# Layer 1's x with tokens on partitions: transposes of 32x32 squares on VectorE and transfers within SBUF in place of TensorE transposes

## The chip, the cores and the metric

The kernel runs on one core of one Trainium2 chip. TensorE multiplies matrices out of SBUF into PSUM; VectorE (DVE), ScalarE (ACT) and GpSimd (POOL) work elementwise on SBUF and PSUM; SyncE (SP) issues transfers, which 16 DMA engines carry out. SBUF has 128 partitions. The engines run side by side, each in the order of its own queue, and wait for one another by semaphores. The metric is the device time of one execution in microseconds, the median over several runs.

## The reference

Four layers are applied one after another to x of shape (4, 512, 32, 32) in float32: 4 images of 512 channels and 1024 tokens. Layers 0, 2 and 3 are attention layers (8 heads, one head, 4 heads) with a residual. Layer 1, which the change touches, is linear attention:

```
Q = einsum('bcn,mc->bmn', xf, wq) + bq          # m = 64 features
K = einsum('bcn,mc->bmn', xf, wk) + bk
V = einsum('bcn,oc->bon', xf, wv) + bv
gate = (max(xf, -1) + mean(xf, -1))[:, :, None]
V = gate * V
Qf = softplus(Q).transpose(0, 2, 1);  Kf = softplus(K)
KV = einsum('bmn,bcn->bmc', Kf, V)
norm = 1 / einsum('bnm,bm->bn', Qf, sum(Kf, -1) + EPS)
wval = einsum('bnm,bmc,bn->bcn', Qf, KV, norm).reshape(b, c, h, w)
return x + gamma * wval
```

## The kernel before, in words

`plain_path` does the whole computation; a second path, `general_path`, follows only when a check of magnitudes at the end fails, and the change leaves it alone. An image lies in SBUF as 128 partitions x 4 chunks x 1024 tokens: channels on partitions. Two images fit at a time; `away` writes one to DRAM and `back` fetches one, both on SP's queue.

Layer 0 runs image by image: `project_qkv` (lines 707 and 832 of the matmul helpers, products of 2x2 blocks by seven multiplications), then `attention`. Layer 1 of image b-1 has no stage of its own. `linear_attention` returns a list of small steps, and `project_qkv` of image b takes one step from that list at each `slot()`, between its own matmuls. The first three images are treated so while Layer 0 projects the next image; Layer 1 of the fourth image rides on the first stage of Layer 2. TensorE's order is written out by hand through this list (`manual_schedule` covers TensorE alone); the order on DVE, ACT, POOL and SP is set by a scheduler when the program is built.

Layer 1 doesn't form V. It uses KV = (Kf x^T) wv^T + (sum of Kf) bv, so it needs x with tokens on partitions, as the moving operand of a product that sums over tokens. The steps of `linear_attention(b, scratch)`, in order:

- `gates`: maximum on DVE (L1414) and sum on ACT (L1417) of each channel; the ACT pass writes four copies nobody reads into scratch buffer 3.
- `features(0)`, `features(1)`: 128 rows of q and k features for 512 tokens each (L641), then `softplus` over both (L1385 to L1391), which uses scratch buffers 0, 1 and 2 as e, u and l. L1389 is the last reader of e, L1390 the last of u, L1391 the last of l.
- `transpose_x(0)` to `transpose_x(3)`: each takes 256 tokens, eight 128x128 transposes on TensorE (L1425) into a PSUM tile of two banks, and one copy to SBUF, on ACT for even pieces (L1432), on DVE for odd ones (L1430). Piece i goes to scratch buffer (i + 3) % 4, so piece 0 takes the one of the gates' copies, and pieces 1, 2 and 3 take e, u and l. `transpose_keys` (L1438) stands between pieces 2 and 3.
- `keys_times_x` (L1454): the product of the transposed keys with pieces 0 and 1 in one step, 2 and 3 in the next; then `sum_keys` (L1465), `divide_queries` (L1478, L1488, L1489, and the transfer L1492 that copies the divided queries to the other 64 partitions), `transpose_kx` (L1497), `keys_times_values` (L641 with wv1, L1513) and two `update` steps (L1520, L1526), which add to x.

For the first three images scratch buffers are the four v tiles of the image being projected, which are written later in the same stage; for the fourth they come from the pool of four pt tiles. `many_tile` is a pool of one tile of 128 x 2048 elements, used by the attention for sums of exponentials. At the start wv1, the weights of V, is loaded by one transfer (L599), 128 partitions x 4 chunks x 512, channel 128 c + p on partition p of chunk c. The attention's quotients pass through DRAM by L1030 and L1033, and L1051 multiplies by them before the projection of the outputs (L1084).

Of the kernel before, what the change touches and what calls it, by code (L numbers as in the profile page):

```python
# [18 lines left out]
P = 128  # L19
# [3 lines left out]
NC = C // P  # L23
NT = S // P
# [2 lines left out]
QT = TB // P  # L27
M = 64
GROUP = 16
LIMIT = 1e18  # L30


# [18 lines left out]
def general_path(ctx: ExitStack, tc: tile.TileContext, d: dict, out: bass.AP):  # L51
# [41 lines left out]
    for b in range(1, B):  # L93
# [19 lines left out]

    gmat = const.tile([P, P // GROUP, GROUP], F32, name="gmat")
    nc.vector.memset(gmat, 1.0 / GROUP)
    nc.gpsimd.affine_select(
        out=gmat, in_=gmat, pattern=[[-GROUP, P // GROUP], [0, GROUP]],
        compare_op=ALU.is_ge, fill=0.0, base=0, channel_multiplier=1,
    )
    nc.gpsimd.affine_select(  # L120
        out=gmat, in_=gmat, pattern=[[GROUP, P // GROUP], [0, GROUP]],
        compare_op=ALU.is_ge, fill=0.0, base=GROUP - 1, channel_multiplier=-1,
    )
# [351 lines left out]
def plain_path(ctx: ExitStack, tc: tile.TileContext, d: dict, out: bass.AP, count):  # L475
# [11 lines left out]
    nc = tc.nc  # L487
# [11 lines left out]
    def acc_tile():  # L499
        return ps_acc.tile([P, TB], F32, tag="acc", name="acc")  # L500

    def two_tile(name):
        return ps_sc.tile([P, 2, TB], F32, tag="sc", name=name)

    def row_tile(name):
        return work.tile([P, TB], F32, tag="row", bufs=3, name=name)
# [7 lines left out]
    def many_tile(name):  # L514
        return work.tile([P, NC, TB], F32, tag="many", name=name)
# [9 lines left out]
    def chunks_tile(tag, name, bufs=1):  # L525
        return work.tile([P, NC, TB], F32, tag=tag, bufs=bufs, name=name)
# [69 lines left out]


    wv1 = chunks_tile("xn", "wv1", 2)
    nc.sync.dma_start(wv1, d["wv1"].rearrange("(c p) o -> p c o", p=P))  # L599
    block1 = chunks_tile("xn", "block1", 2)  # L600
    wqk1 = block1[:, 0, :].rearrange("p (c o) -> p c o", c=NC)
    nc.sync.dma_start(wqk1, d["wqk1"].rearrange("(c p) o -> p c o", p=P))
# [10 lines left out]
    ident = const.tile([P, P], F32, name="ident")  # L613
# [9 lines left out]

    gmat = const.tile([P, P // GROUP, GROUP], F32, name="gmat")
    nc.vector.memset(gmat, 1.0 / GROUP)
# [767 lines left out]
    def linear_attention(b, scratch):  # L1393

        x = xs[b]
        t = {}
        flat = lambda tile: tile.rearrange("p a s -> p (a s)")
# [21 lines left out]
            nc.vector.tensor_scalar(gate, gate, gamma, None, ALU.mult)  # L1419

        def transpose_x(i):
            ps = two_tile("xt")
            for s in range(2):
                for c in range(NC):
                    nc.tensor.transpose(  # L1425
                        ps[:, s, bass.ts(c, P)], x[:, c, bass.ts(2 * i + s, P)], ident
                    )
            t["xt", i] = scratch((i + 3) % 4)
            if i % 2:
                nc.vector.tensor_copy(t["xt", i], ps)  # L1430
            else:
                nc.scalar.copy(t["xt", i], ps)  # L1432

        def transpose_keys():

# [12 lines left out]
        def keys_times_x(i):  # L1448
            if i == 0:
                t["kx"] = acc_tile()  # L1450
            xt = t.pop(("xt", i))

            for s in range(2):
                nc.tensor.matmul(  # L1454
                    t["kx"][s * M : (s + 1) * M, :], lhsT=t["kf"][:, 2 * i + s, :],
                    rhs=xt[:, s, :], start=(i == 0), stop=(i == NT // 2 - 1),
                )
            if i == NT // 2 - 1:
                kx = row_tile("kx")
                nc.scalar.copy(kx, t["kx"])  # L1460
                t["kx"] = kx
# [53 lines left out]
        def update(tb):  # L1515
# [16 lines left out]
            lambda: features(0),  # L1532
            lambda: features(1),
            lambda: transpose_x(0),
            lambda: transpose_x(1),
            lambda: transpose_x(2),
            transpose_keys,
            lambda: transpose_x(3),
            both(lambda: keys_times_x(0), lambda: keys_times_x(1)),
            both(lambda: keys_times_x(2), lambda: keys_times_x(3), sum_keys),  # L1540
            divide_queries,
            transpose_kx,
# [103 lines left out]
    def verdict():  # L1646

        assert next(unit) <= UNITS
        ok = const.tile([P, 2 * UNITS], F32, name="ok")
        nc.vector.tensor_scalar(ok, tops.rearrange("p a n -> p (a n)"), LIMIT, None, ALU.is_le)  # L1650
        row = const.tile([P, 1], F32, name="row")
# [6 lines left out]
    with tc.manual_schedule(engines={mybir.EngineType.PE}):  # L1658
# [73 lines left out]
        for o in range(NC):  # L1732
            ps = gps.get(o)
            if ps is None:
                ps = acc_tile()
# [5 lines left out]
        for o in range(NC):  # L1741
            ps = acc_tile()
# [113 lines left out]
@with_exitstack  # L1856
def conv_seq(ctx: ExitStack, tc: tile.TileContext, d: dict, out: bass.AP):
    nc = tc.nc
    flag = ctx.enter_context(tc.tile_pool(name="flag", bufs=1))
    count = flag.tile([1, 1], mybir.dt.int32, name="count")  # L1860
    plain_path(tc, d, out, count)
    good = nc.values_load(count, min_val=0, max_val=P)
    with tc.If(good < P):
        general_path(tc, d, out)
# [56 lines left out]
```

## Time and profile before

| | |
|---|---|
| median of 3 runs | 2451.55 us (2450.8 to 2452.09) |
| the profiled execution's own time | 2450.76 us |
| its span, first to last instruction | 2449.0 us |
| granted TensorE clock | 1.000 |
| TensorE busy | 2433.3 us, 99% of the span |
| VectorE busy | 1506.1 us, 61% |
| ScalarE busy | 704.6 us, 29% |
| GpSimd busy | 251.1 us, 10% |
| DMA queue of SP's issues | 9.9% of 16 engines' span |
| TensorE's transposes of x (L1425) | 128, 272 to 273 ns each |

The durations come from one profiled execution, whose own time is 0.8 us below the median. Busy time says how full an engine is; matmuls overlap, so the mean length of one (594 ns for 512 columns) is longer than the distance from one to the next, and what a group of them holds TensorE for is read from the starts in the timeline. Issues of transfers are not counted as busy; they are seen as instructions of SPq. A number after an arrow in brackets is the idle time of the engine just before, and what ended it.

### The profile page before, as it was taken

What the parts mean: (1) busy time and instruction counts of PE and PEld (TensorE: products, weight loads), DVE (VectorE), ACT (ScalarE), POOL (GpSimd) and SP (SyncE); (2) the same over time, 40 slices, a digit from 0 to 9 for tenths busy, and PEclk for the clock granted to TensorE, in tenths of its full rate; (3) what the DMA queues carried; (4) which work ended last, traced back from release to release, by engine and by line L of the source; (5) the groups of instructions that cost most, each with busy time, mean ns of one, the idle gap of its engine ahead of it and who ended that gap; (6) DMA issues with size and microseconds to landing.
All of it is one profiled execution on the core that took longest, in us unless ns stands there. A gap on an engine that the chain in (4) does not pass through costs nothing.

```text
span 2449.0 us, 24662 instructions
## 1 busy us (share of the span) xinstructions
PE 2433.3 (99%) x10098; PEld 1225.7 (50%) x10098; DVE 1506.1 (61%) x1798; ACT 704.6 (29%) x864; POOL 251.1 (10%) x240
## 2 busy tenths in 40 slices
PE   9999999999999999999999999999999999999999
PEld 4544544453455344644645446445556456555653
DVE  3677577757775788656595774763554554445344
ACT  1454144415531653221211201112321430332132
POOL 4001100110010001101103021021010001002000
PEclk9999999999999999999999999999999999999999
DMA  5000020002000301011001010110010001001001
GB/s 185 7 12 18 5 78 10 18 5 79 19 9 13 130 23 48 5 69 39 31 1 69 5 74 13 52 69 18 35 69 1 18 35 52 1 35 35 1 22 45
DMA packets 28959, 88.64 MB, mean 36 GB/s; under 512 B 2508, under 2 KB 10188, under 8 KB 25895
## 3 DMA queue, kind: packets, MB, share of 16 engines
q1 hardware_dynamic: 28838, 87.00, 9.9%
q8 instruction: 81, 1.33, 0.2%
q14 instruction: 40, 0.32, 0.0%
HBM read 60.59 MB, written 25.35 MB: 35 GB/s over the span
## 4 chain that ended last, share of the span: by engine, by line
PE 99%; DVE 1%; ACT 0%; issue 0%; DMA 0%; SPq 0%; DVEq 0%
PE acc L707 20%; PE acc L832 12%; PE acc L967 9%; PE acc L982 9%; PE sc L936 9%; PE sc L931 9%; PE acc L839 8%; PE acc L1084 7%; PE acc L1316 6%; PE acc L1277 2%; PE feat L641 1%; PE acc L1018 1%; PE acc L641 1%; PE upd L1520 1%; PE acc L1454 1%; PE xt L1425 1%
## 5 line engine op out<-in xcount | busy, mean ns | idle before, releaser
L941 ACT ACTIVATE pt<-sc 128x1024 f32<-128x1024 f32 x384 | 379.2, 1022 | 541.2 <-PE sc L936 304.0
L950 DVE TENSOR_TENSOR sum<-sum,pt 128x1024 f32<-128x1024 f32 x256 | 314.6, 1229 | 159.0 <-ACT pt L941 146.5
L967 PE MATMUL acc<-pt,v 64*64 64x512 f32 x2048 | 247.6, 591 | 0.0
L931 PE MATMUL sc<-q,k 64*64 64x512 f32 x2048 | 245.0, 591 | 1.1 <-ACT pt L941 1.1
L982 PE MATMUL acc<-pt,v 128*128 128x512 f32 x512 | 240.8, 594 | 0.0
L936 PE MATMUL sc<-q,k 128*128 128x512 f32 x512 | 239.9, 594 | 0.0
L707 PE MATMUL acc<-t,ws 128*128 128x512 f32 x384 | 173.9, 594 | 0.0
L695 POOL TENSOR_TENSOR ws<-wqkv 128x256 f32<-128x256 f32 (+1 forms) x40 | 39.7, 992 | 1307.1 <-PE acc L1018 523.2
L947 DVE TENSOR_TENSOR sum<-pt 128x1024 f32<-128x1024 f32 x64 | 78.0, 1219 | 137.4 <-ACT pt L941 137.4
L982 PEld LDWEIGHTS acc<-pt,v 128*128 128x128 f32 x512 | 96.8, 190 | 125.1 <-issue 121.4
L936 PEld LDWEIGHTS sc<-q,k 128*128 128x128 f32 x512 | 97.1, 191 | 115.9 <-issue 92.7
L967 PEld LDWEIGHTS acc<-pt,v 64*64 64x64 f32 x2048 | 78.3, 133 | 142.5 <-issue 140.3
L931 PEld LDWEIGHTS sc<-q,k 64*64 64x64 f32 x2048 | 77.3, 133 | 140.9 <-issue 131.9
L707 PEld LDWEIGHTS acc<-t,ws 128*128 128x128 f32 x384 | 72.6, 190 | 86.5 <-issue 85.0
L746 ACT COPY v<-acc 128x512 f32<-128x512 f32 x24 | 14.0, 585 | 308.6 <-PE acc L832 308.6
L678 DVE RECIPROCAL rd<-acc 128x512 f32<-128x512 f32 (+1 forms) x24 | 80.5, 3353 | 29.1 <-PE acc L1018 29.1
L832 PE MATMUL acc<-ws,t 128*128 128x256 f32 x384 | 87.3, 380 | 0.0
L839 PE MATMUL acc<-qs,w 128*128 128x512 f32 x192 | 86.6, 593 | 0.0
L839 PE MATMUL acc<-q,ln 128*128 128x512 f32 x192 | 85.8, 593 | 0.0
L1084 PE MATMUL acc<-ot,wo 128*128 128x256 f32 x336 | 80.7, 383 | 2.7 <-ACT ou L1103 2.7
L737 DVE TENSOR_TENSOR v<-acc,v 128x512 f32<-128x512 f32 x72 | 49.5, 689 | 51.5 <-PE acc L832 51.2
L746 ACT COPY q<-acc 128x512 f32<-128x512 f32 x40 | 23.4, 585 | 197.1 <-PE acc L707 197.1
(326 smaller groups left out, 3476.0 us busy)
## 6 DMA issues: line engine op xcount, KB each, us to landing
home<-x SPq DMA_DIRECT2D x8, 2048.0 KB
x<-home SPq DMA_DIRECT2D x8, 2048.0 KB
out<-x SPq DMA_DIRECT2D x32, 256.0 KB
rds<-quotients SPq DMA_DIRECT2D x30, 256.0 KB
rds<-quotients SPq DMA_DIRECT2D x7, 1024.0 KB
x<-in_x SPq DMA_DIRECT2D x3, 2048.0 KB
wo<-in_wo SPq DMA_DIRECT2D x3, 1024.0 KB
w<-in_w SPq DMA_DIRECT2D x1, 3072.0 KB
```

The source lines that it names most:

```text
L678: nc.vector.reciprocal(rd, ps)
L707: nc.tensor.matmul(ps, lhsT=w[:, m, :], rhs=x[:, m, :], start=start, stop=stop, skip_group_check=True)
L832: nc.tensor.matmul(ps[:, bass.ts(r, C // 2)], lhsT=x[:, m, bass.ts(2 * o + r, P)], rhs=w[:, m, :], start=(start and r == 0), stop=stop, sk ...
L839: nc.tensor.matmul(ps, lhsT=x[:, m, bass.ts(o, P)], rhs=w[:, m, :], start=start, stop=stop, skip_group_check=True,)
L931: nc.tensor.matmul(ps[half(h), s, :], lhsT=key(g, i)[half(s), half(h)], rhs=q[qb][half(s), g, :], start=True, stop=True,)
L936: nc.tensor.matmul(ps[:, s, :], lhsT=key(g, 2 * i + s), rhs=q[qb][:, g, :], start=True, stop=True)
L941: exps.append(nc.scalar.activation(pt, ps, AF.Exp, scale=scale).ins)
L950: adds.append(nc.vector.tensor_tensor(acc, acc, pt, ALU.add).ins)
L967: nc.tensor.matmul(outs[qb, g][r][half(s), :], lhsT=v[i // 2][half(r), i % 2, g * P + s * hd : g * P + (s + 1) * hd], rhs=pt[half(r), s, : ...
L982: nc.tensor.matmul(outs[qb, g][0], lhsT=v[j // 2][:, j % 2, bass.ts(g, P)], rhs=pt[:, s, :], start=(j == 0), stop=(j == NT - 1),)
L1084: nc.tensor.matmul(ps[i][:, bass.ts(o, n)], lhsT=w[:, m, bass.ts(o, P)], rhs=t[:, m, :], start=(start and m + o == 0), stop=(stop and m == ...
L1316: nc.tensor.matmul(ps[i, o], lhsT=w[m][:, bass.ts(o, P)], rhs=t[m], start=(start and m == 0), stop=(stop and m == 3), skip_group_check=True,)
```

## The change

`transpose_x` no longer uses TensorE or PSUM. DVE transposes every 32x32 square of 256 tokens x 512 channels in one instruction (4 per image) into half of a `many` tile named squares: pieces 0 and 2 use one half, 1 and 3 the other. A square's transpose stays in the 32 partitions that its channels came from, so SP then issues 16 transfers per piece, each of 32 partitions x 256 elements (32 KB), which put them together in the scratch buffer with 128 tokens on the partitions: 64 transfers per image. The channels and tokens come out in another order than before. `keys_times_x` reads its moving operand in runs of 32 elements for that, and wv1 is loaded in the matching order of rows, by four transfers of 32 partitions in place of one. ACT's and DVE's copies out of PSUM are gone with the transposes.

```diff
--- before.py
+++ after.py
@@ -27,6 +27,7 @@
 QT = TB // P
 M = 64
 GROUP = 16
+SQUARE = 32
 LIMIT = 1e18
 
 
@@ -596,7 +597,10 @@
 
 
     wv1 = chunks_tile("xn", "wv1", 2)
-    nc.sync.dma_start(wv1, d["wv1"].rearrange("(c p) o -> p c o", p=P))
+
+    rows = d["wv1"].rearrange("(c a j) o -> c j a o", c=NC, a=NC)
+    for c in range(NC):
+        nc.sync.dma_start(wv1[c * SQUARE : (c + 1) * SQUARE], rows[c])
     block1 = chunks_tile("xn", "block1", 2)
     wqk1 = block1[:, 0, :].rearrange("p (c o) -> p c o", c=NC)
     nc.sync.dma_start(wqk1, d["wqk1"].rearrange("(c p) o -> p c o", p=P))
@@ -1419,17 +1423,27 @@
             nc.vector.tensor_scalar(gate, gate, gamma, None, ALU.mult)
 
         def transpose_x(i):
-            ps = two_tile("xt")
-            for s in range(2):
-                for c in range(NC):
-                    nc.tensor.transpose(
-                        ps[:, s, bass.ts(c, P)], x[:, c, bass.ts(2 * i + s, P)], ident
-                    )
-            t["xt", i] = scratch((i + 3) % 4)
-            if i % 2:
-                nc.vector.tensor_copy(t["xt", i], ps)
-            else:
-                nc.scalar.copy(t["xt", i], ps)
+
+
+
+
+
+            if i == 0:
+                t["squares"] = many_tile("squares")
+            sq = t["squares"][:, i % 2 * 2 : i % 2 * 2 + 2, :].rearrange(
+                "p b (r n j) -> p (b r) n j", j=SQUARE, n=2 * NC
+            )
+            nc.vector.transpose(
+                sq.rearrange("p r n j -> p n r j"),
+                x[:, :, i * 2 * P : (i + 1) * 2 * P].rearrange("p c (n j) -> p c n j", j=SQUARE),
+            )
+            xt = t["xt", i] = scratch((i + 3) % 4)
+            to = flat(xt).rearrange("p (a f) -> p a f", a=NC)
+            part = lambda i: slice(i * SQUARE, (i + 1) * SQUARE)
+            for r, a in itertools.product(range(NC), range(NC)):
+                nc.sync.dma_start(
+                    to[part(r), a, :], sq[part(a), r].rearrange("p n j -> p (n j)")
+                )
 
         def transpose_keys():
 
@@ -1448,12 +1462,12 @@
         def keys_times_x(i):
             if i == 0:
                 t["kx"] = acc_tile()
-            xt = t.pop(("xt", i))
+            xt = flat(t.pop(("xt", i))).rearrange("p (b s j) -> p s b j", s=2, j=SQUARE)
 
             for s in range(2):
                 nc.tensor.matmul(
                     t["kx"][s * M : (s + 1) * M, :], lhsT=t["kf"][:, 2 * i + s, :],
-                    rhs=xt[:, s, :], start=(i == 0), stop=(i == NT // 2 - 1),
+                    rhs=xt[:, s], start=(i == 0), stop=(i == NT // 2 - 1),
                 )
             if i == NT // 2 - 1:
                 kx = row_tile("kx")
```

Lines of the changed kernel lie 4 higher after the load of wv1 and 14 higher after `transpose_x`.

## The prediction

> **What bounds the kernel now.** I read the page's busy times and its chain first, then TensorE's waits, then the timeline of one Layer 1 stage, then the list of SP's DMA issues.
>
> ```profile
> PE 2433.3 (99%) x10098; PEld 1225.7 (50%) x10098; DVE 1506.1 (61%) x1798; ACT 704.6 (29%) x864; POOL 251.1 (10%) x240
> ...
> PE 99%; DVE 1%; ACT 0%; issue 0%; DMA 0%; SPq 0%; DVEq 0%
> ```
>
> TensorE is busy for 2433.3 of 2449.0 us and the chain that ended last is 99% TensorE. So whatever leaves its queue is a gain of its full length, and whatever makes its queue wait is a loss of its full length; nothing else counts. The waits of TensorE amount to about 10 us over the whole run, none of them in Layer 1.
>
> The timeline of the second image's projection (Layer 1 of the first image rides on it), columns start, length, engine, line, operation:
>
> ```profile
> 218.61 1.29 DVE L1051 TENSOR_TENSOR ot<-ot,rds 128x512 f32<-128x512 f32 x2 [1.01 <-DMA rds<-quotients]
> 220.23 1.89 PE L1084 MATMUL acc<-ot,wo 128*128 128x256 f32 x8
> 240.64 0.18 ACT L1417 ACTIVATION_READ_ACCUMULATOR v<-x 128x1 f32 x1
> 251.46 0.69 DVE L1387 TENSOR_SCALAR v<-v 128x1024 f32<-128x1024 f32 x1 [0.46 <-ACT v L1386]
> 253.83 1.22 DVE L1389 SCALAR_TENSOR_TENSOR v<-v,v 128x1024 f32<-128x1024 f32 x1 [1.08 <-ACT v L1388]
> 260.02 1.04 PE L1425 MATMUL xt<-ident,x 128*128 128x128 f32 x8
> 260.89 3.60 PE L707 MATMUL acc<-t,ws 128*128 128x512 f32 x8
> 273.00 1.94 PE L1454 MATMUL acc<-v,kf 128*64 128x512 f32 x8
> 278.50 1.94 PE L1454 MATMUL acc<-v,kf 128*64 128x512 f32 x8
> 280.37 0.43 PE L1465 MATMUL ksum<-ones,kpart 128*128 128x64 f32 x2
> ```
>
> A group of eight transposes holds TensorE from 260.02 until L707 at 260.89: 0.87 us, not 8 x 0.27. L1454 reads the transposed x: pieces 0 and 1 from 273.00, pieces 2 and 3 from 278.50, piece 3 half way to 280.37, at 279.4. L1389 is the last reader of the buffer that takes piece 1.
>
> SP's own issues (start, length), and its line L1492 with min/median/max in ns:
>
> ```profile
> 211.84 0.54 SPq L1030 DMA_DIRECT2D quotients<-rd  x1
> 213.62 1.23 SPq L1033 DMA_DIRECT2D rds<-quotients  x2
> 316.91 0.34 SPq L573 DMA_DIRECT2D home<-x  x1
> ```
>
> ```profile
> L1492 SPq DMA_DIRECT2D block<-block x4: 517/520/527, 295.8 to 1032.4; - x4
> ```
>
> One issue costs SP 0.32 to 0.34 us for a large transfer over 128 partitions (L573), 0.52 for 64 partitions within SBUF (L1492), 0.53 for 4 partitions (L1030), about 0.6 for 64 partitions out of DRAM (L1033, two in 1.23). This is the number on which the case turns.
>
> [...] Here L1033 could start at 213.62, 1.78 us after L1030 began, so some 1.3 us after an issue ends. [...]
>
> **The change part by part.**
>
> 1. Removed from TensorE: 4 images x 4 groups x 0.87 = 13.9 us, 3.48 per image. Eight ACT copies (1.0 us) and eight DVE copies (1.22) go too; ACT is 29% busy, worth nothing.
>
> 2. Added on DVE: 16 transposes of 128x1024. Not in the trace; [...] nearest row the 1024-element copy, 1.22. [...] I take 1.22. In the build's order of DVE's queue, the first two of an image stand among the four L686-L689 and so ahead of L1051, which L1084 on TensorE waits for. 2.44 us meet DVE's 1.01 idle and the 0.33 between L1051's end (219.90) and L1084 (220.23): TensorE is 1.1 us late, in three images. In the last image they stand among the L950 sums, between a reciprocal and L1051, where ACT's exponentials wait for DVE: 0 to 2 us, taken as 1.
>
> 3. Added on SP: 64 issues per image, 16 per piece, each 32 partitions of 1 KB, all in one in-order queue. Shape not in the trace. Low end 0.33 (the 128-partition rows), high end 0.68 (longest L1033). I take the nearest row, within SBUF and below 128 partitions, 0.52, plus 0.04 between issues: a pitch p = 0.56. [...]
>
> 4. The chain that follows, first three images (times as in the fence). Piece 0's buffer is free after the gates' copies at 240.8: issued until 240.8 + 16 x 0.56 = 249.8, landed 251.1. The third DVE transpose reuses the half of the squares that piece 0 leaves, so it waits until 251.1 and ends at 252.3. Queued behind it on DVE are L780 and L1387; L1387 ends at 253.6 instead of 252.15, ACT's Ln then starts at 253.65 instead of 252.74, and L1389 ends at 256.0 instead of 255.05. Only then may piece 1 be issued, and pieces 2 and 3 follow without a pause: 48 x 0.56 = 26.9, last issue at 282.9, landed 284.2. The fourth transpose waits for piece 1's landing (about 266) and is not late. TensorE wants piece 3 at 279.4 in the old clock, 275.9 without its transposes. It stands from 275.9 to 284.2, with all else behind it. Piece 3 is used 4.8 us later than before, though 3.48 us were saved. With point 2, +5.9 per image, 17.7 for three.
>
> 5. Last image:
>
> ```profile
> 992.01 1.23 DVE L1389 SCALAR_TENSOR_TENSOR l<-l,l 128x1024 f32<-128x1024 f32 x1 [1.66 <-ACT l L1388]
> ...
> 1012.35 1.94 PE L1454 MATMUL acc<-l,kf 128*64 128x512 f32 x8
> ```
>
> L1389 ends at 993.2; 993.2 + 26.9 + 1.3 = 1021.4 against 1013.3 for piece 3: +8.1, with point 2 +9.1.
>
> 6. Counted at nothing. wv1 by four issues at the start: SP has nothing else until 117.70 and wv1 is first read at 297; without that cover three issues, 2 us. L1492, home<-x and x<-in_x queue behind the 64 issues: before, L1492 starts at 295.8, 13 us after SP would be free. L1454 now reads x in runs of 32: no row shows such a moving operand; [...] I take 0[...].
>
> Sum: 17.7 + 9.1 = +26.8 us. The profiled execution took 2450.76 us (span 2449.0), giving 2477.6; the median of the runs is 0.8 above it, so 2478. In general the change is 192 p - 80.7 us: zero at p = 0.42.
>
> **The rivals.**
>
> *Issue is cheap* (other side). If 32-partition transfers issue like the large ones, 0.34 + 0.04 = 0.38, piece 3 lands at 256.0 + 18.2 + 1.3 = 275.5, before 275.9: nothing stands, and three images gain 3.48 - 1.1 = 2.4 each; the last loses 0.4. Together -6.7: 2444. For it: L573, and L1060 and L1097 near 0.33 to 0.37 with small rows. Against: every row below 128 partitions is 0.49 or more, but for none is the partition count shown to be the cause. It decides below p = 0.42.
>
> *Issue is dearer, or landing is.* At L1033's 0.634 the formula gives +41, and piece 0 lands 1.2 us later, which holds the third transpose: +3.6, so 2496. At 0.72 it is +57.5 and 3 x 2.5: 2516. [...] For it: startup issues of 1.2 to 5 us (L544, L599, L606), behind megabytes of loads. [...]
>
> *Hidden anyway, about equal*: p of 0.40 to 0.44 brings savings and stalls level, 2446 to 2456. That the transposes stay on TensorE is excluded: the built order has none.
>
> **How the numbers follow.** Forecast (p from 0.44 to 0.65, some 2456 to 2498): 0.64. Dearer: 0.20. About equal: 0.06. Cheap: 0.10. Slower by over 0.2% (4.9 us, about what a measurement of this kernel can tell from no change): 0.84; within it 0.06; faster 0.10. The likeliest is 2478. The range 2452 to 2505 leaves out the cheap case, part of the equal one and the upper half of the dear one.
>
> **What would show it.** Right: no xt group; TensorE idle 7 to 9 us per image before the later L1454 (about 12 in the last), released by DMA; SP in an unbroken row of some 48 issues at 0.56; busy TensorE time down by about 14 us while the span grows. Wrong: issues at 0.38 and no wait at L1454; a wait at an earlier place (L1084 beyond 1 us, or L1454's first call at 269.5), or a DVE transpose above 2 us; L1454 itself longer than 0.43 us a step.

## The result and the profile after

The changed kernel takes 2508.14 us (median of 4 runs, 2506.21 to 2509.84) against 2451.18 us (2450.40 to 2452.09) for the kernel before, with one run more than in the table above: a ratio of 1.0232, 95% interval 1.0214 to 1.025. It is slower by 57 us, where +26.8 us had been forecast and a range up to 2505 given. The direction and the place are as forecast; the size is more than twice it.

The page of the changed kernel: busy times of the engines, then the shares of the chain that ended last.

```profile
PE 2434.4 (97%) x9970; PEld 1212.3 (48%) x9970; DVE 1511.5 (60%) x1806; ACT 697.4 (28%) x856; POOL 245.3 (10%) x240
...
PE 90%; SPq 5%; DVE 2%; issue 1%; ACT 1%; DMA 1%; DVEq 0%
```

The span is 2506.2 us instead of 2449.0. The chain, 99% TensorE before, now holds SP's issues (SPq) with 5%. The first number is the surprise: 128 matrix instructions worth 13.9 us are gone, yet TensorE is busy for 1.1 us longer than before. Some of the rest must run slower.

What TensorE waited for (total, times, longest, in us). None of these rows was there before:

```profile
PE acc L1468 <- DMA v<-squares: 34.8, 6, 9.3
PE acc L1468 <- DMA l<-squares: 13.0, 2, 8.2
PE acc L711 <- DVE k L743: 5.7, 3, 1.9
PE acc L711 <- DVE q L784: 1.2, 1, 1.2
```

L1468 is `keys_times_x` (L1454 before): 47.8 us of waits for the pieces of the transposed x, two in each image, for pieces 2 and 3. The longer is always the one for piece 3. L711 waits for k and q, tiles of the image being projected, which DVE writes.

The instructions that touch the squares (min/median/max in ns): SP's transfers and DVE's transposes.

```profile
L1444 SPq DMA_DIRECT2D v<-squares x192: 507/589/1556, 239.2 to 791.1; - x192
...
L1444 SPq DMA_DIRECT2D v<-squares x3: 590/592/603, 239.2 to 240.4; - x3
...
L1436 DVE STREAM_TRANSPOSE squares<-x x16: 1232/1237/1246, 212.3 to 1046.5; 128x1024 f32<-128x1024 f32 x16
```

DVE's transpose costs 1.24 us, as estimated (1.22). The issue costs SP 0.59 us in the median, and from one to the next pass 0.63. The second line shows the first three issues of the first image alone: SP had issued nothing since 213.2, so nothing of its own was under way any more (the DMA share is 0.00 from 230 to 239.15), and they already take 0.59 to 0.60.

The chain of waits through the first image (start, length), shortened in the long row of issues:

```profile
248.68 1.88 DMA v<-squares
...
251.15 0.96 issue
252.11 0.65 DVE k L784
252.76 0.68 DVE v L1391
253.47 1.06 ACT v L1392
254.56 1.37 DVE v L1393
...
256.49 0.59 SPq L1444
...
286.65 1.87 DMA v<-squares
288.98 1.98 PE acc L1468 x4
```

This is step 4 of the prediction link by link: piece 0 lands, the third DVE transpose waits for it ("issue", then L784 queued behind it), softplus's L1391, L1392 and L1393 are late, and only when L1393 has let go of its buffer does SP issue the 48 transfers of pieces 1 to 3, in an unbroken row. SP's row runs from 255.94 to 287.24: a mean pitch of 0.652 us, a little above the usual 0.63 because a few issues took longer, one of them 1.29. Piece 3 is usable 1.74 us after the last issue ended.

TensorE's timeline there (all times in this trace lie 1.70 us earlier than before, since the start of the program was shorter by that much):

```profile
278.88 1.08 PE L1468 MATMUL acc<-v,kf 128*64 128x512 f32 x4 [3.56 <-DMA v<-squares]
288.98 1.98 PE L1468 MATMUL acc<-v,kf 128*64 128x512 f32 x4 [9.02 <-DMA v<-squares]
...
291.37 3.27 PE L711 MATMUL acc<-t,wqkv 128*128 128x512 f32 x4
294.47 1.88 PE L711 MATMUL acc<-x,ws 128*128 128x512 f32 x4
```

After the wait for piece 2 the four instructions take 1.08 us; after the 9-us wait the same four take 1.98, and the next four of L711 take 3.27 instead of 1.9. At 294.47 all is as usual. The table by stretches says why (columns: length, busy time of PE, PEld, DVE, ACT, POOL with instructions, then the granted clock, DMA share, GB/s):

```profile
286.00:288.98 2.98, 0.00 (x1) 0.03 (x1) 0.00 (x0) 0.00 (x0) 0.00 (x0) 0.50 0.18 44
288.98:291.37 2.39, 2.39 (x7) 0.78 (x7) 0.00 (x0) 0.38 (x1) 0.00 (x0) 0.50 0.00 0
291.37:294.50 3.13, 3.13 (x6) 1.34 (x7) 0.28 (x2) 0.21 (x1) 0.00 (x0) 0.57 0.01 3
294.50:300.00 5.50, 5.50 (x18) 2.65 (x17) 3.26 (x3) 0.00 (x0) 0.00 (x0) 1.00 0.00 0
```

The granted clock is 0.50 at the end of the wait and stays there for 5.0 us of work; in the other three images for 6.0 to 6.1. It had fallen by 280.50 (0.89 from 280.00 to 280.50, 0.50 from there to 281.00), half a microsecond after piece 2's four products: these 1.08 us of work between two waits did not keep it up. A case further below has a clock of 0.52 to 0.58 after an idle time of only 1.9 us. The prediction had no such term.

### The profile page after: what moved, and what is told of

Same layout as the page of the kernel before. It is cut to its first block, busy times and chain, and to the rows that moved or that the text cites. A ratio compares the mean times of both kernels' runs of the same rounds, so it can differ in the third digit from the quotient of the medians.

```text
span 2506.2 us, 24825 instructions
## 1 busy us (share of the span) xinstructions
PE 2434.4 (97%) x9970; PEld 1212.3 (48%) x9970; DVE 1511.5 (60%) x1806; ACT 697.4 (28%) x856; POOL 245.3 (10%) x240
## 4 chain that ended last, share of the span: by engine, by line
PE 90%; SPq 5%; DVE 2%; issue 1%; ACT 1%; DMA 1%; DVEq 0%
PE acc L711 15%; PE acc L836 11%; PE acc L971 9%; PE acc L986 9%; PE sc L940 9%; PE sc L935 9%; PE acc L843 8%; PE acc L1088 7%; PE acc L1320 6%; SPq L1444 5%; PE acc L1281 2%; PE acc L1022 1%; PE acc L645 1%; PE upd L1534 1%; PE kv L645 1%
## 5 line engine op out<-in xcount | busy, mean ns | idle before, releaser
L711 PE MATMUL acc<-t,ws 128*128 128x512 f32 x384 | 174.3, 594 | 0.0
L711 PEld LDWEIGHTS acc<-t,ws 128*128 128x128 f32 x384 | 73.0, 191 | 88.9 <-issue 87.2
L1088 PE MATMUL acc<-ot,wo 128*128 128x256 f32 x336 | 80.6, 383 | 2.7 <-ACT ou L1107 2.7
L836 PEld LDWEIGHTS acc<-ws,t 128*128 128x128 f32 x384 | 73.0, 190 | 11.2 <-issue 1.4
## 6 DMA issues: line engine op xcount, KB each, us to landing
out<-x SPq DMA_DIRECT2D x32, 256.0 KB
rds<-quotients SPq DMA_DIRECT2D x30, 256.0 KB
```

Source lines behind the costliest of these rows:

```text
L711: nc.tensor.matmul(ps, lhsT=w[:, m, :], rhs=x[:, m, :], start=start, stop=stop, skip_group_check=True)
L836: nc.tensor.matmul(ps[:, bass.ts(r, C // 2)], lhsT=x[:, m, bass.ts(2 * o + r, P)], rhs=w[:, m, :], start=(start and r == 0), stop=stop, sk ...
L1088: nc.tensor.matmul(ps[i][:, bass.ts(o, n)], lhsT=w[:, m, bass.ts(o, P)], rhs=t[:, m, :], start=(start and m + o == 0), stop=(stop and m == ...
```

## The experiments

Three theories were set against each other for the waits. The issue theory is the prediction's: SP's own time per transfer times the number of transfers. The transfer theory says that the bytes under way, or the number of rows they are cut into, set the time. The buffer theory says that only the late release of softplus's buffers costs. Diffs are against the changed kernel unless said otherwise; ratios are to the kernel before.

**Half as many transfers, same bytes.**

```
-            for r, a in itertools.product(range(NC), range(NC)):
+            for r, a in itertools.product(range(NC), range(0, NC, 2)):
                 nc.sync.dma_start(
-                    to[part(r), a, :], sq[part(a), r].rearrange("p n j -> p (n j)")
+                    to[part(r), a : a + 2, :].rearrange("p a f -> p (a f)"),
+                    sq[part(a), r // 2 * 2 : r // 2 * 2 + 2].rearrange("p r n j -> p (r n j)"),
```

> Changed kernel, but 8 transfers of 32 partitions by 512 numbers per piece instead of 16 of 256: the same bytes in 32 issues per image instead of 64. The 32-row blocks of x that are moved end up on other partitions than they should, so the sums over tokens (keys times x) are of the wrong channels; all times stay comparable. Issue theory (SP's own time per transfer, 0.63 to 0.65 us, times the number of transfers sets when piece 3 is there): piece 0's issues end 5 us earlier, so the third DVE transpose does not wait and e is free at about 254.3 us; 24 issues x 0.65 = 15.6 us, landing 1.7 us, so piece 3 is there at about 271.6, before the 275.3 at which TensorE first wants piece 2. No wait at keys times x in any image, granted clock 1.00 throughout, and the 13.9 us of the removed transposes become a gain: about 2438 us. Transfer theory (the bytes, or the small rows in flight, set the time): the wait of 9 us stays, about 2508 us. Buffer theory (what costs is only that pieces 1 to 3 must wait for softplus's buffers): e is free 1.6 us earlier and the rest stays, about 2503 us.

A transfer has 32 rows as before, twice as long, so the number of rows is halved too. Measured: 2439.62 us, ratio 0.9958 (0.9944 to 0.9972), 1.6 us from what the issue theory said. The page's busy times, SP's transfers and the wait that is left:

```profile
PE 2419.1 (99%) x9970; PEld 1207.5 (50%) x9970; DVE 1513.0 (62%) x1806; ACT 697.4 (29%) x856; POOL 250.8 (10%) x240
...
L1444 SPq DMA_DIRECT2D v<-squares x96: 507/589/1472, 239.4 to 739.0; - x96
...
PE acc L1469 <- DMA l<-squares: 0.3, 1, 0.3
```

An issue of twice the bytes costs the same 589 ns, and with half of them the 47.8 us of waits become 0.3. What is left is the gain: TensorE is busy for 14.2 us less than before. The strided operand of the keys' products thus costs nothing to speak of (their group of eight takes 1.94 us here as before), and DVE's transposes, which are all still there, cost little: the span gains 2.6 us less than the busy time (11.6 against 14.2), of which 1.2 are the wait for q.

The two spans also split the loss. Of 2506.2 - 2437.4 = 68.8 us, 47.5 are waits at L1468, 5.7 waits for k at L711, and 15.3 lie in TensorE's busy time for the same instructions: together 68.5.

**Twice as many transfers, same bytes.**

```
-            for r, a in itertools.product(range(NC), range(NC)):
+            for r, a, h in itertools.product(range(NC), range(NC), range(2)):
                 nc.sync.dma_start(
-                    to[part(r), a, :], sq[part(a), r].rearrange("p n j -> p (n j)")
+                    to[part(r), a, h * P : (h + 1) * P], sq[part(a), r, h * NC : (h + 1) * NC].rearrange("p n j -> p (n j)")
```

> Changed kernel, but 32 transfers of 32 partitions by 128 numbers per piece: the same bytes in 128 issues per image instead of 64. Issue theory: piece 0's 32 issues end 10.3 us later, the third DVE transpose and with it softplus's last reader of e follow some 9 us later, and then 96 issues x 0.65 = 62.6 us instead of 31.3: about 40 us more per image, some 2660 us (2630 if the last image is only 31 us late and the pitch is 0.60). Transfer theory with the bytes as the limit: about 2508 us, the pitch halves to about 0.32. Buffer theory: at most the 9 us by which e comes free later, 4 x 9, about 2540 us.

Measured: 2639.3 us, ratio 1.0774 (1.0756 to 1.0792), 131 us above the changed kernel, or 32.8 per image. SP's row and DVE's third transpose in the first image:

```profile
239.46 81.88 SPq L1444 DMA_DIRECT2D v<-squares  x128
...
252.45 1.23 DVE L1393 SCALAR_TENSOR_TENSOR v<-v,v 128x1024 f32<-128x1024 f32 x1 [1.08 <-ACT v L1392]
262.18 1.25 DVE L1436 STREAM_TRANSPOSE squares<-x 128x1024 f32<-128x1024 f32 x1 [3.60 <-DMA v<-squares]
```

128 issues in 81.88 us are 0.640 each, at half the bytes. The forecast of 2660 was 20 us too high: in this build L1393 stands ahead of the third transpose on DVE and is not late at all. The row simply runs through: 81.88 us in the first image against 48.09, its pause included, in the changed kernel, 33.8 longer; in the last image 48 issues more, 48 x 0.64 = 30.7. Measured are 32.8 in the mean. The buffer theory is out, and so is the transfer theory as far as it speaks of bytes. The number of rows, doubled here and halved in the run before, is told apart by the runs with two queues.

**Buffers that are free early.**

```
-            xt = t["xt", i] = scratch((i + 3) % 4)
+            if i == 1:
+                t["room"] = work.tile([P, NC, TB], F32, tag="rds", name="room")
+            if i == 0:
+                xt = scratch(3)
+            elif i < 3:
+                xt = t["room"][:, 2 * i - 2 : 2 * i, :]
+            else:
+                xt = work.tile([P, 2, TB], F32, tag="ou", name="room")
+            t["xt", i] = xt
```

> Changed kernel, but pieces 1 and 2 go into the halves of the buffer for the quotients' rows (free in Layer 1) and piece 3 into one of the ou buffers, so that no transfer waits for softplus's e, u or l; only the squares (two halves) and SP's row of issues hold them. Issue theory: the 64 issues run nearly unbroken from when the first is free to go; without the 6.7 us in which SP now waits for e (249.3 to 255.9), piece 3 lands some 6 to 7 us earlier, so that about 5.5 of the 12.6 us of waits of the first three images stay and those of the last vanish: 2465 to 2475 us. Buffer theory: all waits at keys times x vanish, about 2438 us. Transfer theory: as the issue theory here, since it too counts from the first transfer.

Measured: 2453.36 us, ratio 1.0011 (1.0004 to 1.0018), 12 us better than the lower end of that forecast. SP's issues in the first image:

```profile
220.28 10.71 SPq L1452 DMA_DIRECT2D room<-squares  x16
240.17 10.32 SPq L1452 DMA_DIRECT2D v<-squares  x16
250.59 20.88 SPq L1452 DMA_DIRECT2D room<-squares  x32
```

The 64 issues cost as much as ever, 41.9 us, but 16 of them now go at 220, before the gates, which the forecast had missed. The row ends at 271.5 instead of 287.2, ahead of TensorE's need. So an early start hides the row as well as a shorter row does; this run alone does not tell issue and buffer theory apart, the two before it do. Its span, 2452.6, is 15.2 us above that of the run with half the transfers: waits for k are 6.3 of it, one wait of 2.6 for a late piece in the last image follows, and TensorE's busy time for the same instructions is 6.9 us longer, at a mean clock of 0.997 instead of 0.999. The times of this kernel vary with that clock (2447.99 to 2457.05): its three executions at a clock of 1.000 have spans of 2446.3 to 2446.5, 8.9 to 9.1 us above the run with half the transfers, which is the two waits and no more.

**Two queues for pieces 1 to 3.**

```
-                nc.sync.dma_start(
+                (nc.scalar if a % 2 and i else nc.sync).dma_start(
```

> Changed kernel, but of pieces 1 to 3 every other transfer is issued by ACT instead of SP: 24 issues on each after e is free instead of 48 on SP; buffers, bytes and the moment of release are the same. Issue theory: two queues halve the row, about 16 us from 255.9 (ACT's part behind its copy of the keys a little later, about 273.6 landed), so nothing waits any more at pieces 2 and 3: about 2440 us, up to 2455 if ACT's later copy of the keys delays the first matmuls of keys times x. Transfer theory: the same bytes and rows in flight, about 2508 us. Buffer theory: about 2508 us.

Measured: 2458.59 us, ratio 1.0032 (1.0022 to 1.0042): just outside the forecast. The first three images go as the issue theory has it, with no wait at L1468. Left are:

```profile
PE acc L711 <- DVE k L743: 5.7, 3, 1.9
PE acc L1468 <- DMA l<-squares: 5.5, 1, 5.5
```

The waits for k had been in the changed kernel all along and the forecast forgot them; they do not depend on pieces 1 to 3. That the same bytes, in the same buffers, released at the same moment, are there in time in these three images from two queues shows that neither the bytes nor the number of rows under way are the limit. The DMA engines are far from full too: their share is 0.18 in the stretch 286.00 to 288.98 above. And since the first issues of a row, with nothing under way, cost the same 0.59 to 0.60 us, the time belongs to the single issue and not to a queue that backs up.

**Piece 0 on two queues too.**

```
-                nc.sync.dma_start(
+                (nc.scalar if a % 2 else nc.sync).dma_start(
```

> As the run with pieces 1 to 3 on two queues, with piece 0's transfers too divided between SP and ACT (8 each). Theory for what is left in that run (the third DVE transpose waits until piece 0 has landed and holds k behind it on DVE, so TensorE waits 1.9 us for k and restarts slowly, in three images; and 5.5 us at piece 3 in the last): piece 0 lands 5 us earlier, the three waits for k (5.7 us) and their slow restarts (about 4) vanish, the last image's wait shrinks to between 0 and 5.5: 2442 to 2450 us. Rival (k is late because of DVE's added transposes themselves, 1.24 us each, not because of the landing): the three waits for k stay, about 2455 to 2459 us.

Measured: 2440.55 us, ratio 0.9961 (0.9946 to 0.9976). Transfers by queue, and the third DVE transpose:

```profile
L1444 SPq DMA_DIRECT2D v<-squares x96: 507/592/1918, 240.4 to 741.4; - x96
L1444 ACTq DMA_DIRECT2D v<-squares x96: 517/602/1623, 240.4 to 741.4; - x96
...
247.34 1.25 DVE L1436 STREAM_TRANSPOSE squares<-x 128x1024 f32<-128x1024 f32 x1 [2.52 <-DMA v<-squares]
```

ACT issues at the same 0.60 us as SP, and the two rows run at the same time. The third transpose starts 7.0 us after SP's row begins instead of 11.8; no wait for k and none at L1468 on a transfer is left. So k was late because of piece 0's landing, not because of DVE's added work. This one edit makes the slow kernel faster than the one before. SP's time for its row of issues, with the waits and the slow clock that follow from it, made the whole loss: the two kernels, with the same transfers of 32 KB, are 67.6 us apart.

**Products that nobody reads, put into the waits.**

```
+            if i >= 2:
+                ps = two_tile("fill")
+                for n in range(4 * i - 4):
+                    nc.tensor.matmul(
+                        ps[:, n % 2, :], lhsT=ident, rhs=x[:, n % NC, bass.ts(0, TB)],
+                        start=True, stop=True,
+                    )
```

> Changed kernel, with matrix products nobody reads put into the waits on TensorE: 4 (of 128x512, 0.94 us each) ahead of piece 2's products and 8 ahead of piece 3's, in each image. They wait for nothing that is late, and take 3.8 and 7.5 us in waits of 1.6 to 4.8 and 8.2 to 9.3 us. Restart theory (of the 68.8 us by which the changed kernel's span exceeds that of the kernel with half the transfers, 47.5 are waits at keys times x, 5.7 waits for k, and the other 15.3, all in TensorE's busy time, come from TensorE running slowly for some us after a wait): with TensorE kept busy until piece 3 lands most of those 15.3 vanish, so although 48 products more are computed the kernel gets faster: 2494 to 2502 us, mean clock above 0.99, the four L711 products after keys times x at 1.9 instead of 3.3 us. Rival (the slow products after the wait come from something else, such as the strided x or transfers under way): 2508 us or more, and the products stay at 3.3 us.

Measured: 2498.22 us, ratio 1.0197 (1.0181 to 1.0212): with 48 products more, 9.9 us less than the changed kernel. First image again:

```profile
281.70 7.13 PE L1469 MATMUL fill<-x,ident 128*128 128x512 f32 x16
289.36 1.08 PE L1474 MATMUL acc<-v,kf 128*64 128x512 f32 x4 [0.53 <-DMA v<-squares]
...
290.64 1.94 PE L711 MATMUL acc<-t,wqkv 128*128 128x512 f32 x4
```

SP's row and piece 3's landing are where they were (TensorE goes on at 289.36 instead of 288.98), but the products behind it take 1.08 and 1.94 us instead of 1.98 and 3.27. The restart theory holds: the slow products come from the idle time before them, and cost 9.9 / 4 = 2.5 us per image on the path. Both waits are filled here, so this run does not tell which of the two lets the clock fall.

**By way of DRAM: 20 issues per image, twice the bytes.**

```
-            for r, a in itertools.product(range(NC), range(NC)):
-                nc.sync.dma_start(
-                    to[part(r), a, :], sq[part(a), r].rearrange("p n j -> p (n j)")
-                )
+            home = dram.tile([P, NC, 2 * P], F32, tag="squares", bufs=4, name="home_sq")
+            nc.sync.dma_start(home, sq.rearrange("p r n j -> p r (n j)"))
+            rows = home.rearrange("(a p) r f -> r p a f", a=NC)
+            for r in range(NC):
+                nc.sync.dma_start(to[part(r)], rows[r])
```

> Changed kernel, but each piece goes by one store of the squares to DRAM (128 partitions, 4 KB each) and four loads of 32 partitions by 4 by 256 numbers: 20 issues per image instead of 64, twice the bytes. The stores wait for no buffer of softplus, so the squares come free early; from e's release at about 254.3 there are 12 loads and a store to issue, 13 x 0.6 = 8 us[...]: piece 3 there by about 265, before the 275.3 wanted. Issue theory: no wait at keys times x, none for k, clock 1.00, the 13.9 us of the removed transposes are gained: 2437 to 2441 us. Transfer theory: twice the bytes by way of DRAM must cost, 2508 us or more. Rival (a load at the head of SP's queue waits for its store to land[...], and the queue with it): [...] hidden in the first three images, at most 2445 us.

Measured: 2440.00 us, ratio 0.996 (0.9946 to 0.9973), the best time beside the run with half the transfers. Loads and stores:

```profile
L1447 SPq DMA_DIRECT2D v<-home_sq x48: 302/430/1730, 240.9 to 731.3; - x48
L1444 SPq DMA_DIRECT2D home_sq<-squares x16: 320/332/591, 214.1 to 960.7; - x16
```

There is no wait for the squares or for any piece anywhere. A load takes SP 0.43 us, a store 0.33, and the stores wait for no buffer of softplus. The feared wait of a load for its store does not show: in the first image the last store is issued at 242.9 and the loads of pieces 1 to 3 go from 253.9.

**Pieces 2 and 3 by TensorE.** For i of 2 and 3 the code of the kernel before runs, with the channels written into the columns in the order that wv1 now has (`keys_times_x` reads these two pieces without runs again; that part is left out here):

```
+            if i >= 2:
+                ps = two_tile("xt")
+                for s in range(2):
+                    cols = ps[:, s, :].rearrange("p (a c j) -> p c a j", a=NC, c=NC)
+                    for c in range(NC):
+                        nc.tensor.transpose(cols[:, c], x[:, c, bass.ts(2 * i + s, P)], ident)
...
```

> Changed kernel, but pieces 2 and 3 are transposed by TensorE as in the kernel before (copied by ACT and DVE) and only pieces 0 and 1 by DVE and transfers: 32 issues per image, of which 16 after e is free. No third and fourth DVE transpose, so nothing waits for piece 0's landing and e is free at about 253. Issue theory: piece 1 lands at 253 + 16 x 0.65 + 1.7 = 265.1, before the 266 to 270 at which TensorE first wants it; half of the 13.9 us is gained and nothing is lost: 2443 to 2446 us. Rival (piece 1 is wanted with piece 0 in the first group of keys times x and is 1 to 3 us late in each image, with a slow restart behind it): 2450 to 2458 us.

Measured: 2445.52 us, ratio 0.9982 (0.9974 to 0.9989), as the issue theory had it. The mean clock is 1.00, and TensorE's group of keys times x that needs piece 1 follows without a wait, as does the later one:

```profile
269.90 1.94 PE L1484 MATMUL acc<-v,kf 128*64 128x512 f32 x8
```

Half of the transposes gone is 4.8 us gained, all of them gone some 10: the gain does scale with what leaves TensorE, once nothing waits.

**What makes an issue dear.** The prediction left open why rows with few partitions cost more. Two runs, each of a single execution, use the run by way of DRAM as a ruler, with all extra issues hidden; their diffs are against that run. First the stores, cut differently for each piece:

```
-            nc.sync.dma_start(home, sq.rearrange("p r n j -> p r (n j)"))
+            src = sq.rearrange("p r n j -> p r (n j)")
+            size = (P, 64, SQUARE, P)[i]
+            for lo in range(0, P, size):
+                for r0, r1 in [(0, NC)] if i < 3 else [(0, 2), (2, NC)]:
+                    nc.sync.dma_start(home[lo : lo + size, r0:r1], src[lo : lo + size, r0:r1])
```

> As the run by way of DRAM, whose issues are all hidden, used as a ruler for one issue on SP: piece 0's store is one of 128 partitions (4 KB rows), piece 1's two of 64 partitions, piece 2's four of 32, piece 3's two of 128 partitions with 2 KB rows. Partition theory (an issue is dear because it spans fewer than 128 partitions; 0.33 us was seen for 128, 0.52 for 64 and 0.59 for 32): 0.33, 0.52, 0.59 and 0.33 us. Place theory (an issue is dear because both ends are in SBUF): all near 0.33 us. Bytes theory: 0.33 us and then less for each of the smaller ones. The time of the kernel should stay at 2440 to 2442 us in each case.

Measured (2440.53 us): the answers for the stretches in which pieces 0, 1, 2 and 3 of the first image are stored.

```profile
L1448 SPq DMA_DIRECT2D home_sq<-squares x1: 352/352/352, 214.8 to 214.8; - x1
...
L1448 SPq DMA_DIRECT2D home_sq<-squares x2: 495/546/597, 219.3 to 219.9; - x2
...
L1448 SPq DMA_DIRECT2D home_sq<-squares x4: 338/422/428, 234.8 to 236.1; - x4
...
L1448 SPq DMA_DIRECT2D home_sq<-squares x2: 338/384/430, 243.7 to 244.1; - x2
```

Bytes are out: a quarter of them costs more, not less. The partition theory fails too: 32 partitions are cheaper (0.42) than 64 (0.55), and far from 0.59. The kernel's time does not notice.

Then copies within SBUF beside the stores:

```
+            if i == 1:
+                t["room"] = flat(work.tile([P, NC, TB], F32, tag="rds", name="room"))
+            size = (0, P, 64, SQUARE)[i]
+            for lo in range(0, P, size) if i else ():
+                src = sq[lo : lo + size].rearrange("p r n j -> p (r n j)")
+                nc.sync.dma_start(t["room"][lo : lo + size, : 4 * 2 * P], src)
+            for lo in range(0, P, SQUARE) if i == 3 else ():
+                src = sq[lo : lo + SQUARE, 0].rearrange("p n j -> p (n j)")
+                nc.sync.dma_start(t["room"][lo : lo + SQUARE, 4 * 2 * P : 5 * 2 * P], src)
```

> As the run by way of DRAM, with copies of the squares within SBUF beside it that nobody reads, all hidden: piece 1's as one transfer of 128 partitions (4 KB rows), piece 2's as two of 64, piece 3's as four of 32, and piece 3's again as four of 32 with 1 KB rows, the shape of the changed kernel's. After the ruler on stores to DRAM (0.34, about 0.55, about 0.42 us for 128, 64 and 32 partitions), the question is whether SBUF at both ends makes an issue of 32 partitions dear. Place theory: 128 and 64 partitions 0.5 or more, 32 partitions 0.59, with either row length. Rival (place is nothing; the 0.59 came from the shape or from the many transfers one after another): 0.34, 0.55 and 0.42 as to DRAM, and the last four 0.59 if the 1 KB rows are the cause, 0.42 if it was the long row of issues. The kernel's time stays at 2440 to 2443 us in each case.

Measured (2440.09 us): one issue of 128 partitions, two of 64, four of 32, and the sixteen with 1 KB rows of all images.

```profile
L1451 SPq DMA_DIRECT2D room<-squares x1: 538/538/538, 220.8 to 220.8; - x1
...
L1451 SPq DMA_DIRECT2D room<-squares x2: 522/610/697, 235.5 to 236.0; - x2
...
L1451 SPq DMA_DIRECT2D room<-squares x4: 589/590/596, 244.4 to 246.3; - x4
...
L1454 SPq DMA_DIRECT2D room<-squares x16: 512/588/597, 260.4 to 969.3; - x16
```

The place theory holds for 128 and 32 partitions: within SBUF the 128 partitions take 0.54 us instead of 0.33 to 0.35 and the 32 take 0.59 instead of 0.42, whatever the row length. For 64 partitions the difference is small (0.61 against 0.55), so place is not the only thing that counts. One to four issues stand behind each of these figures, but the second image repeats them within SBUF (0.53, two in 1.25, 0.59). What in SP's work makes it so is not shown by any run.

## Why the prediction was wrong

**Right.** Step 1: the removed work is worth what was said; TensorE's busy time falls by 14.2 us (13.9 said) where nothing waits. The transposes on DVE cost 1.24 us (1.22). Step 4 named the chain that decides, and every link of it is in the trace: landing of piece 0, third transpose, softplus's last reader, a row of 48 issues, landing, TensorE's wait. Step 6: the strided operand, wv1's four loads and SP's later issues cost nothing that shows. The waits stand at the second group of keys times x, released by DMA, as forecast; their length was not right in the first three images: 12.6, 11.7 and 10.5 us instead of 7 to 9 (in the last 13.0 instead of 12).

**Step 3 failed: the pitch.** It took the nearest row, 0.52 us for L1492, plus 0.04. That row was from the right place, within SBUF, but of 64 partitions; 32 cost 0.59, and the pitch is 0.652 in the first image and 0.647 in the last (31.06 us for 48 issues). The upper bound of 0.68 was no bound either: in the trace before, L1030 took up to 0.74. The rival "dearer" had 0.634 and above and got a chance of 0.20. With the measured pitch the prediction's own formula gives 192 x 0.652 - 80.7 = +44.5, with piece 0's later landing 3 x 1.5 more: about 2500 us. So the pitch is most of the error, and some 8 us are left for the other terms. Of the landing, 1.3 was said (the two lines behind it give 1.24); 1.7 was measured in the first image.

**Step 4's release of softplus's buffer** was predicted at 256.0 in the old clock, 254.3 in that of the changed kernel. L1393 ended at 255.91, 1.6 us later, because piece 0's sixteen issues have the same dear pitch (10.1 us) and the landing comes after them. In the second and third image the release is 1.6 us later than forecast too, counted from the shift that the image began with.

**Point 2 failed in kind.** It had TensorE 1.1 us late at L1084 in three images. DVE's L1055 does run 1.08 us later than before (217.99 against 218.61 in a clock that is 1.70 ahead), but TensorE's L1088 starts at 218.54 while L1055 is still busy, exactly when it would have without the change, so its first products do not read what L1055 writes:

```profile
217.99 1.25 DVE L1055 TENSOR_TENSOR ot<-ot,rds 128x512 f32<-128x512 f32 x2
218.54 1.89 PE L1088 MATMUL acc<-ot,wo 128*128 128x256 f32 x8
```

That one ended and the other began 0.33 us apart before was a coincidence that had been read as a dependence. In the last image the 1 us is real, but sits elsewhere: 1.2 us at L711 for q.

**A term was missing: the restart.** The prediction counted a wait of TensorE as "a loss of its full length; nothing else counts". But after each wait of 8.2 to 9.3 us the granted clock was 0.50 for another 5.0 to 6.1 us of work; filling the wait with other work gives 9.9 us back, 2.5 per image.

The sum with measured terms, in us by which the image's x leaves for DRAM later than before (the first `home<-x` issue; differences from image to image, 1.70 added for the earlier start):

| | images 1 to 3, each | last image |
|---|---|---|
| predicted | +5.9 | +9.1 |
| point 2, not there | -1.1 | |
| release 1.6 later | +1.6 | |
| pitch, 48 x 0.092 and 48 x 0.087 | +4.4 | +4.2 |
| landing, 1.74 and 1.48 instead of 1.3 | +0.4 | +0.2 |
| restart | +2.5 | +2.5 |
| sum | +13.7 | +16.0 |
| measured | +13.76, +13.39, +13.93 | +16.59 |

The restart's 2.5 is the mean of the run with filled waits. The waits for k (5.7 us) do not appear in the sum: without them TensorE would only have reached piece 3's wait sooner. The largest single error is the pitch, 17.4 us over four images; the restart is 10 and the release 4.8.

The sign was never in doubt in these runs: the zero at a pitch of 0.42 is far from 0.65. What takes the loss away is fewer issues in one queue behind the release, as in the runs with half the transfers, with piece 0 too on two queues, and by way of DRAM; with nothing late, all three are 0.4% faster than the kernel before. (The run with half the transfers leaves out the right order of the blocks and shows the time only; the other two can replace the changed kernel.)

## What to carry to other kernels

When a transpose is moved off the busiest engine, count the issues behind the last buffer that comes free. Here 48 of them in one queue, at 0.65 us each, turned a saving of 14 us into a loss of 57; half as many, two queues, or 20 larger transfers per image by way of DRAM left a gain of about 10 us, and a row that could start early (its end at 271.5 instead of 287.2) brought the ratio back to 1.0011. For the pitch, take the dearest row of the same place and as few partitions (within SBUF, 64 partitions took 0.52 us in the trace before and 32 took 0.59), and divide the row among queues or make the transfers larger before anything else. The waits of 8.2 to 9.3 us on TensorE, with the clock at 0.50 behind them, cost 2.5 us per image more than their length (by the run with filled waits), so look at the granted clock behind a wait and add the slow products to its price. And when two rows of a timeline follow each other closely, check that the later one reads what the earlier one writes before pricing a delay.

## What had not been expected of the hardware

Within SBUF the issue of a transfer cost SP the same 589 ns in the median for 32 partitions of 512 B, 1 KB or 2 KB; it differed with place and number of partitions instead, and not in one direction: 0.33 to 0.35, 0.55 and 0.42 us for 128, 64 and 32 partitions to DRAM, 0.54, 0.61 and 0.59 within SBUF.

Behind a wait of 1.9 us TensorE's clock was near one half in two of the three stretches below and full in the other. They are the stretches behind the waits for k in the first and the third image of the changed kernel, then behind that in the first image of the run with filled waits:

```profile
256.72:258.51 1.79, 1.79 (x4) 0.84 (x5) 1.79 (x3) 0.00 (x0) 0.00 (x0) 1.00 0.23 58
...
761.18:764.26 3.08, 3.08 (x5) 1.28 (x6) 2.78 (x3) 0.00 (x0) 0.00 (x0) 0.58 0.16 37
```

```profile
257.04:260.47 3.43, 3.43 (x5) 1.37 (x5) 2.78 (x3) 0.00 (x0) 0.00 (x0) 0.52 0.17 43
```

After waits of 1.90, 1.90 and 1.89 us the granted clock is 1.00, 0.58 and 0.52; the first two come from the same execution. Why they differ is not settled here.
